# Routing and expert slots moved inside both arms of attention's branch, with their data in used halves of q, k and v

## The chip, the core and the metric

The kernel runs on one core of one Trainium2 chip. A core has a matrix engine (PE, TensorE), a vector engine (DVE, VectorE), an activation engine (ACT, ScalarE), a general engine (POOL, GpSimd) and a sequencer that issues transfers (SP, SyncE). Each works through its own list of instructions in order; semaphores tie the lists together. SP, ACT and POOL can issue DMA transfers, which sixteen DMA engines carry out. SBUF is the memory that the engines compute from, PSUM holds the products of PE, DRAM holds inputs, outputs and some scratch.

The metric is device time in microseconds (us), lower is better.

## The reference

The input is an image of 256 channels and 64 x 64 pixels, so 4096 tokens. Layer 0 is a windowed linear attention over the image and takes about the first 1000 us; the change leaves it alone. Layer 1 is:

```python
# --- layer 1 ---
t = _to_tokens(x)                                  # 4096 tokens x 256
t = t + attn(_ln_t(t))                             # 8 heads of 32, softmax over all 4096 keys
t = t + ffn(_ln_t(t))
x = _from_tokens(t, x)

def ffn(x):                                        # 8 experts, 256 -> 1024 -> 256
    logits = xt @ Wr + br
    probs = softmax(logits); top_p, top_idx = top_k(probs, 2)
    weights = top_p / top_p.sum(-1)
    xe = layernorm(xt) * ln_g[e] + ln_b[e]
    h = gelu(xe @ W1[e] + b1[e]); y = h @ W2[e] + b2[e]
    out = (weights[..., None] * y[of the two chosen experts]).sum(1)
```

Only the two chosen experts of a token are computed: the kernel sorts the tokens by expert on the chip ("routing") and runs the experts on groups of rows ("slots").

## The kernel before, in words

**Attention** stands in one arm of a branch, `with tc.If(tame > 0)` (L1271), taken when the scores are small enough for exponentials without a maximum; the `Else` arm holds a slower, safer attention. In the arm there are 16 rounds of 32 steps. A round is one chunk of 512 queries (`qc`, 8 of them) and one group of four heads (`g`, 2 of them); a step is one tile of 128 keys. In a step PE computes scores for four heads (`scores`, L1326) into one bank (`ps_one`) and a set of three (`ps_three`, two such sets in turn, `three_banks()`); ACT takes the exponential of the one bank (L1335) and of the three (L1338) into a buffer of 128 x 2048, of which there are eight; two steps later PE multiplies it with the values (`value_sums`, L1285). The softmax denominators need the sum of all these buffers: DVE adds most of them up (L1357), and every fourth buffer is added by a DMA from POOL instead (`pe<-pe`, L1346). A buffer is free again three steps after its own when DVE adds it, six steps when the DMA does. At the start of the next round DVE copies the finished sums out of PSUM (`take`, L1369); later steps of the next round pack the denominators, send them through DRAM (SP), and scale the result (L1407). In every odd round, at steps 13 and 25, two tiles each go through the output projection (`some_projections`, L1263), whose results DVE adds to the tokens `t` (L1267), with the statistics of the next layer norm.

**Early routing** (`early_routing`, L951) routes the first 12 tiles of tokens to four "early" slots, the first 256 of the rows for each of four experts, while attention still runs. Its data lie in the half of the queries that attention no longer needs. It is a list of parts: load; norms; top one; top two; count (two products with constant matrices on PE, in a `three_banks()` turn of their own, L1014, copied by DVE, L1016); ranks; places; one-hot tables; invert (24 small matmuls, again a turn of its own, L1042, copied at L1049); finish; and six parts that write the normed rows to DRAM (`zrows`). The table `when` (L1418) gives each part a whole step, `(8, 13), (8, 21), (8, 25), (9, 9), ...`; `tc.issue_after(latest[0])` puts it behind DVE's last add.

**After the branch** both arms meet, and a second part opens new pools (L1519): constants (L131) and the row `br` are loaded, the full routing runs on DVE, POOL and PE (two_norms, logits, best, counts L1715, ranks, one-hots L1803 to L1826), and the slots run beside it, dealt out by `advance(n)`, which takes `n` steps of the generator `run`. There are four early slots, 28 full ones of 256 rows and four half ones, 36 in all. For a slot, `load` fetches the expert's `cols`, `W1`, `W2`, `b2` through SP (L1566 to L1569, three buffers for the weights) and its rows through POOL (`xs`, an indirect gather, L1587); `enter` transposes them (L1602) and applies gain and shift (L1607 on ACT, L1611 on DVE); then 8 x 2 products with `W1` (L1632), Gelu on ACT (L1635), 2 x 8 products with `W2` (L1648), the bias on DVE (L1652), and an indirect scatter to `yrows` in DRAM (L1653). Slots beyond the usual number stand in a second branch, `If(more_slots)`, that is not taken here. The ending loads the two results of each token (`y<-yrows`, L1869), weighs and adds them, transposes (L1879) and stores the image.

No planner decides the order in attention: it is the order of the calls, shifted by `issue_after`. Each engine's list is in that order, and everything behind the branch's end waits for everything in it.

Of the kernel before, what the change touches and what calls it, by code (L numbers as in the profile page):

```python
# [30 lines left out]
P = 128  # L31
# [85 lines left out]
def tile_conv_attn_hybrid(ctx: ExitStack, tc: tile.TileContext, a: dict, out: bass.AP):  # L117
# [27 lines left out]
    class Norm:  # L145
# [8 lines left out]
        def stats(self, i):  # L154
            st6 = self.pool.tile([P, 6], F32, tag="st6", name="st6", bufs=2)
            nc.vector.bn_stats(st6, t[:, i, :C])
            nc.vector.bn_aggr(self.mv[:, i, :], st6)
# [735 lines left out]
    def rsqrts(x, y, part):  # L893
        bits = y.bitcast(I32)
        nc.vector.tensor_single_scalar(bits, x.bitcast(I32), 1, op=ALU.arith_shift_right)
        nc.vector.tensor_scalar(bits, bits, -1.0, float(0x5F3759DF), op0=ALU.mult, op1=ALU.add)
        for _ in range(3):
            nc.vector.scalar_tensor_tensor(part, y, -0.5, y, op0=ALU.mult, op1=ALU.mult)
            nc.vector.tensor_mul(part, part, x)
            nc.vector.scalar_tensor_tensor(y, part, 1.5, y, op0=ALU.add, op1=ALU.mult)  # L900

    def two_norms(first, last, x, y, part, less):
        mean, var = (z[:, first:last] for z in (norm2.mean, norm2.var))
        nc.vector.tensor_scalar_add(x[:, 0], var, 1e-5)
        nc.vector.scalar_tensor_tensor(x[:, 1], x[:, 0], 1e-5, var, op0=ALU.mult, op1=ALU.add)
        rsqrts(x, y, part)
        nc.vector.scalar_tensor_tensor(less, mean, -1.0, y[:, 1], op0=ALU.mult, op1=ALU.mult)

    def logits(to, first, last, rstd, br):
        shape = [P, last - first, NE]  # L910
        on_experts = lambda v: v.unsqueeze(2).to_broadcast(shape)
        on_tiles = lambda v: v.unsqueeze(1).to_broadcast(shape)
        nc.vector.tensor_mul(to, on_experts(norm2.mean[:, first:last]), on_tiles(wr_sum))
        nc.vector.tensor_sub(to, t[:, first:last, C:], to)
        nc.vector.tensor_mul(to, to, on_experts(rstd))
        nc.vector.tensor_add(to, to, on_tiles(br))

    def best(hot, most, first, place, logit, rank):
        shape = list(logit.shape)
        on_experts = lambda v: v.unsqueeze(2).to_broadcast(shape)  # L920
        nc.vector.tensor_reduce(most, logit, AX.X, ALU.max)
        nc.vector.tensor_tensor(first, logit, on_experts(most), ALU.is_equal)
        nc.vector.tensor_mul(first, first, rank.unsqueeze(1).to_broadcast(shape))
        nc.vector.tensor_reduce(place, first, AX.X, ALU.max)
        nc.vector.tensor_tensor(hot, first, on_experts(place), ALU.is_equal)

    def without(logit, hot):
        nc.vector.scalar_tensor_tensor(logit, hot, -1e30, logit, op0=ALU.mult, op1=ALU.add)

    def positions(hot, row, at, pos, whole, part, within, which, off):  # L930
        nc.vector.tensor_mul(at, hot, row.rearrange("p e i -> p i e"))
        nc.vector.tensor_reduce(pos, at, AX.X, ALU.add)
        if off:
            nc.vector.tensor_scalar_add(whole, pos, off)
        else:
            nc.vector.tensor_copy(whole, pos)
        nc.vector.tensor_single_scalar(part, whole, P - 1, op=ALU.bitwise_and)
        nc.vector.tensor_copy(within, part)
        nc.vector.tensor_single_scalar(whole, whole, 7, op=ALU.arith_shift_right)
        nc.vector.tensor_copy(which, whole)  # L940

    def rows_of(source, target, low, high, got, second, spare, spares):
        nc.vector.scalar_tensor_tensor(got, high, float(P), low, op0=ALU.mult, op1=ALU.add)
        nc.vector.tensor_scalar(second, got, N + 1.0, -float(N), op0=ALU.is_ge, op1=ALU.mult)
        nc.vector.tensor_add(second, second, got)
        nc.vector.tensor_scalar(source, second, -1.0, 0.0, op0=ALU.add, op1=ALU.max)
        nc.vector.scalar_tensor_tensor(spare, got, 0.0, spares, op0=ALU.is_equal, op1=ALU.mult)
        nc.vector.tensor_add(spare, spare, got)
        nc.vector.tensor_scalar_add(target, spare, -1.0)

    def early_routing(spaces, banks):  # L951

        M, E = ETILES, EARLY
# [14 lines left out]

        names = ["rank", "iota", "before", "ones", "number", "high", "base", "spare_early"]
# [28 lines left out]

        def norms():
            two_norms(0, M, x, y, part, less)  # L1000

        def top_one():
            logits(logit, 0, M, y[:, 0], br)
            best(hots[0], most, one, place, logit, c["rank"])

        def top_two():
            without(logit, hots[0])
            best(hots[1], most, one, place, logit, c["rank"])
            nc.vector.tensor_add(chosen.rearrange("p e i -> p i e"), hots[0][:, :, :E], hots[1][:, :, :E])
# [71 lines left out]
    with ExitStack() as phase:  # L1081
# [382 lines left out]
        with branch.Else():  # L1464


            with (
# [48 lines left out]
                for part in early_routing([qk[:, 0, g, :] for g in range(KC)], lambda n: [one_bank() for _ in range(n)]):  # L1516
                    part()

# [391 lines left out]
```

## Time and profile before

| | us |
|---|---|
| median of the runs (3) | 2788.68 |
| lowest, highest | 2784.85, 2788.74 |
| the profiled execution | 2792.98 |
| its span, first to last instruction | 2791.2 |
| granted clock of PE, mean | 0.981 |
| attention's steps (first to last exponential of the 16 rounds) | 1110 to 2212 |
| PE's first transposes of slot 0 | 2230.3 |
| last products of a slot | 2746 |

| engine | busy us | share |
|---|---|---|
| PE | 2666.9 | 96% |
| DVE | 1873.2 | 67% |
| ACT | 1512.3 | 54% |
| POOL | 817.1 | 29% |

A line of the profile in order of time reads: start, length, engine, line of the kernel, operation, what it writes and reads, the shapes, how many instructions it groups, and in brackets how long the engine sat idle before it and what ended that ("issue": nothing that the profile shows). A line of the table of stretches gives the busy time of each engine between two times. Busy shares are means over the whole kernel; a stage is read by its own rows. PEclk is the clock that PE was granted, in parts of full speed.

### The profile page before, as it was taken

Reading aid. Unit: us, or ns where it says so; the run is one execution under the profiler, and the core shown is the slowest. Engines: PE = TensorE matmul, PEld = TensorE weight load, DVE = VectorE, ACT = ScalarE, POOL = GpSimd, SP = SyncE. Lnnn points to the kernel's source line nnn. Section 1 sums busy time; section 2 is a strip of 40 time slices with the busy share of each in tenths; the row PEclk is TensorE's granted clock in tenths of the full one; section 3 lists DMA queues with packets and bytes.
Section 4 is the critical chain, followed back from the end, with each engine's and each line's share of the span. In section 5 each row is a group of like instructions: output and inputs, shape, how many; then the busy total and the mean of one; then the engine's idle time right before and its main releaser. Section 6 shows DMA issues by size and latency. Waiting matters only on the chain. (4 is left out here: it accounts for less than half of the span.)

```text
span 2791.2 us, 72155 instructions
## 1 busy us (share of the span) xinstructions
PE 2666.9 (96%) x31106; PEld 1221.1 (44%) x31106; DVE 1873.2 (67%) x2518; ACT 1512.3 (54%) x2110; POOL 817.1 (29%) x918
## 2 busy tenths in 40 slices
PE   6889999988999999999999999999999899999996
PEld 5454336645433655111212121212121278888884
DVE  6758688565878875888888888898888741111114
ACT  3322323222332334999898988898989642222222
POOL 2057777404877741000000100000000112222220
PEclk9999999999999999999999999999999999999996
DMA  5000000000000000555555555555655455665665
GB/s 143 6 23 25 11 28 21 8 12 23 22 13 28 21 21 1 107 111 118 109 121 109 116 111 111 105 117 105 128 118 117 97 196 190 209 198 197 212 211 191
DMA packets 120990, 266.04 MB, mean 95 GB/s; under 512 B 20659, under 2 KB 81817, under 8 KB 106581
## 3 DMA queue, kind: packets, MB, share of 16 engines
q0 software_dynamic: 22368, 133.18, 22.7%
q1 hardware_dynamic: 91124, 119.20, 13.1%
q10 hardware_dynamic: 7168, 8.92, 0.9%
q8 instruction: 248, 4.06, 0.6%
q14 instruction: 82, 0.66, 0.1%
HBM read 127.81 MB, written 18.12 MB: 52 GB/s over the span
## 5 line engine op out<-in xcount | busy, mean ns | idle before, releaser
L1326 PE MATMUL ps_three<-qk 32*64 32x512 f32 x6144 | 564.9, 614 | 3.2 <-DVE t L1267 1.3
L1326 PE MATMUL ps_one<-qk 32*64 32x512 f32 x2048 | 560.0, 614 | 0.2 <-ACT pe L1335 0.2
L1357 DVE TENSOR_TENSOR act<-act,pe 128x2048 f32<-128x2048 f32 x195 | 446.8, 2291 | 87.0 <-ACT pe L1338 53.4
L642 ACT COPY sm<-ps_sc 128x384 f32<-128x384 f32 (+3 forms) x454 | 218.4, 510 | 526.9 <-PE ps_sc L822 338.6
L1338 ACT ACTIVATE pe<-ps_three 128x1536 f32<-128x1536 f32 x330 | 477.4, 1447 | 0.0
L649 DVE TENSOR_TENSOR sm<-ps_sc,mask 128x512 f32<-128x512 f32 (+3 forms) x740 | 340.0, 519 | 68.8 <-PE ps_sc L822 65.6
L649 POOL TENSOR_TENSOR sm<-sm,mask 128x192 f32<-128x192 f32 (+3 forms) x428 | 349.6, 846 | 113.7 <-ACT sm L642 113.3
L1357 DVE TENSOR_TENSOR act<-act 128x2048 f32<-128x2048 f32 x150 | 344.8, 2299 | 55.5 <-ACT act L1338 42.0
L1346 POOL DMA_DIRECT2D pe<-pe x108 | 92.9, 860 | 949.6 <-ACT pe L1338 675.6
L1285 PE MATMUL ps_acc<-pe,v 128*32 128x512 f32 x2640 | 353.2, 607 | 0.0
L1635 ACT ACTIVATE hid<-ps_hp,cols 128x256 f32<-128x256 f32 (+1 forms) x288 | 133.0, 462 | 349.5 <-PE ps_hp L1632 347.6
L1326 PEld LDWEIGHTS ps_three<-qk 32*64 32x64 f32 x6144 | 112.8, 130 | 416.9 <-ACT pe L1335 242.2
L1338 ACT ACTIVATE act<-ps_three 128x1536 f32<-128x1536 f32 x182 | 263.2, 1446 | 0.0
L1632 PE MATMUL ps_hp<-xe,w 128*128 128x256 f32 (+1 forms) x1152 | 247.9, 371 | 0.0
L1648 PE MATMUL ps_yp<-w,hid 128*128 128x256 f32 x1088 | 241.1, 379 | 0.0
L822 PE MATMUL ps_sc<-qk 32*64 32x384 f32 (+3 forms) x3584 | 234.6, 458 | 0.1
L1335 ACT ACTIVATE pe<-ps_one 128x512 f32<-128x512 f32 x330 | 197.3, 598 | 61.3 <-PE ps_one L1326 37.1
L649 POOL TENSOR_TENSOR sm<-sm,ycut 128x384 f32<-128x384 f32 (+4 forms) x146 | 147.2, 1029 | 257.3 <-ACT sm L642 256.9
L1632 PEld LDWEIGHTS ps_hp<-xe,w 128*128 128x128 f32 x1152 | 201.8, 191 | 39.8 <-ACT hid L1635 5.2
L1648 PEld LDWEIGHTS ps_yp<-w,hid 128*128 128x128 f32 x1088 | 204.2, 190 | 26.5
L838 PE MATMUL ps_acc<-sm,v 128*32 128x256 f32 (+3 forms) x2688 | 213.3, 419 | 0.1
L1285 PE MATMUL ps_acc<-act,v 128*32 128x512 f32 x1456 | 193.9, 604 | 2.3 <-DVE act L1369 2.3
(335 smaller groups left out, 2882.0 us busy)
## 6 DMA issues: line engine op xcount, KB each, us to landing
pe<-pe POOLq DMA_DIRECT2D x108, 1024.0 KB
w<-in_L_ffn_W SPq DMA_DIRECT2D x72, 1024.0 KB
by<-recs SPq DMA_DIRECT2D x48, 256.0 KB
b<-in_L_ffn_b SPq DMA_DIRECT2D x36, 128.0 KB
rows<-in_x SPq DMA_DIRECT2D x16, 256.0 KB
y<-yrows SPq DMA_DIRECT2D x8, 512.0 KB
y<-yrows ACTq DMA_DIRECT2D x8, 512.0 KB
rec<-recs SPq DMA_DIRECT2D x60, 64.0 KB
```

Source lines behind the costliest of these rows:

```text
L642: copied = nc.scalar.copy(sm[:, :used], sc[:, :used])
L649: done = engine.tensor_mul(to, of, mk.unsqueeze(1).to_broadcast(list(to.shape)))
L822: nc.tensor.matmul(scs[h][u : u + rows, at : at + n], kT[hs[h], P * i + u : P * i + u + rows], qT[hs[h], CH * ix + CELL * c0 : CH * ix + C ...
L838: nc.tensor.matmul(acc[hs[h], CELL * c0 : CELL * c1], v[:, i, hs[h]], sms[h][:, at : at + n], start=not begun[0], stop=last and at == plac ...
L1285: nc.tensor.matmul(to[D * hd : D * (hd + 1), :], lhsT(hd), rhs(hd), start=start, stop=stop, skip_group_check=True,)
L1326: nc.tensor.matmul(to[CELL * u : CELL * (u + 1), :], qk[hs, 1, g, P * i + CELL * u : P * i + CELL * (u + 1)], qk[hs, 0, g, chunk(qc)], sta ...
L1335: first = nc.scalar.activation(head(pe, 0), one, AF.Exp, scale=C**-0.5)
L1338: nc.scalar.activation(pe[:, CH:], three.rearrange("p h n -> p (h n)"), AF.Exp, scale=C**-0.5).ins
L1357: latest[:] = [nc.vector.tensor_add(total, total, weights_of[r, i]).ins]
L1632: nc.tensor.matmul(hp[:, :n], w1[:, k, tok(m)], x_now[:, k, :n], start=k == 0, stop=k == KC - 1)
L1635: done["gelu"] = nc.scalar.activation(hid[:, m, :n], hp[:, :n], AF.Gelu, bias=cols[:, m : m + 1]).ins
L1648: product = nc.tensor.matmul(yp, hid[:, m, tok(j)], w2[:, m, :], start=m == 0, stop=m == NH - 1)
```

## The change

1. Routing and the slots leave the second part and become `route_and_run`, called inside both arms. Constants, `br`, the routing's small tiles and PSUM pools open there. The code stands twice in the program.
2. The slots' tiles no longer come from a pool. They are cut from q, k and v by `cutter`: three pairs of weights in the keys of group 0, the first four chunks of queries, and the keys of group 1; `xs`, `xe`, `b2`, `cols`, the lists of rows and the flags in query chunks 4 to 6; `hid` and `y` in the values. `next_of` rotates them. The ending's image lies in `act`.
3. `run` yields once after the loads of slot 0 and once after those of slot 1, before any PE work. These two yields are taken in attention's last round, at steps 0 and 29, behind `turned[0]`, the last small transfer of a round's reciprocals. The early slots' loads keep the order of SP's queue (`issue_after(done["weights"])`), and an early slot's bias comes ahead of its weights.
4. Early routing is cut into pieces of one or a few operations with a cost each, and dealt to rooms: steps 1, 9, 13, 17, 21 and 25 of rounds 8 to 14, each with so many us. A piece stands behind DVE's last add and behind `take`'s copy or the projection's last statistic. Count and inversion go into the third bank of a projection's set; the count's two results leave in one copy.
5. The flag `more_slots` is read behind the branch's end, after all slots.

```diff
-    with ExitStack() as phase:
-        wts = pool("m_wts", 1)
-        small = pool("m_small", 1)
-        cst.update(constants_of("m", wts))
-        br = row_on_all("L1_ffn_br", NE, wts)
...
-            w1 = work.tile([P, KC, HID], F32, name="w1", bufs=3)
-            w2 = work.tile([P, NH, C], F32, name="w2", bufs=3)
...
+        for_early = [qk[:, 0, g, : 4 * CH] for g in range(KC)]
+        of_keys = [(qk[:, 1, g, : 4 * CH], qk[:, 1, g, 4 * CH :]) for g in range(KC)]
+        of_queries = cutter([qk[:, 0, g, 4 * CH : 7 * CH] for g in range(KC)])
+        of_values = cutter([v.rearrange("p i c -> p (i c)")])
+        rotating = {
+            "w": [of_keys[0], for_early, of_keys[1]],
+            "xs": [of_queries(C) for _ in range(4)],
+            "xe": [of_queries(KC, SLOT) for _ in range(2)],
+            "b2": [of_queries(C) for _ in range(2)],
+            "cols": [of_queries(NH + 2 * KC) for _ in range(2)],
+            "hid": [of_values(NH, SLOT) for _ in range(2)],
+            "y": [of_values(C) for _ in range(4)],
+        }
+        def next_of(name):
+            rotating[name].append(rotating[name].pop(0))
+            return rotating[name][-1]
...
+                in_order = slot[0] and "weights" in done
+                with tc.issue_after(done["weights"]) if in_order else nullcontext():
+                    *of, done["weights"] = weights(slot)
...
+            ahead = [load(slots[0])]
+            yield
+            ahead.append(load(slots[1]))
+            yield
+            (ps,) = slot_ps
+            xe = enter(ahead[0], slots[0][0] is not None)
...
+        def route_and_run(work_on, slot_ps, beside, done):
+            with ExitStack() as experts:
+                wts, small = pool("m_wts", 1), pool("m_small", 1)
+                slot_ps.append(experts.enter_context(psum("m_ps", 2)))
+                cst.update(constants_of("m", wts))
+                br = row_on_all("L1_ffn_br", NE, wts)
...
-                when = [(8, 13), (8, 21), (8, 25), (9, 9), (9, 21), (10, 9), (10, 13), (10, 21), (10, 25), (11, 9), (11, 21), (12, 9)]
-                when += [(12, 13), (12, 21), (12, 25), (13, 9), (13, 21), (14, 9)]
-                early = dict(zip(when, early))
+                load_early, pieces = early_routing(for_early)
+                early, shared = {(8, 1): [load_early]}, {}
+                slots = [
+                    (r, i, room)
+                    for r in range(8, len(rounds) - 1)
+                    for i, room in ((1, 2.2), (9, 0.7), (13, 0.95), (17, 0.8), (21, 0.95), (25, 0.95))
+                ]
+                r, i, room = slots.pop(0)
+                for cost, ops in pieces:
+                    if cost is None:
+                        while not (r % KC == KC - 1 and i in (13, 25)) or (r, i) in early:
+                            r, i, room = slots.pop(0)
+                        shared[r, i] = ops
+                        r, i, room = slots.pop(0)
+                        continue
+                    if cost > room:
+                        r, i, room = slots.pop(0)
+                    room -= cost
+                    early.setdefault((r, i), []).extend(ops)
...
-                        some_projections(2)
+                        behind = some_projections(2, shared.get((r, i)))
...
                     if (r, i) in early:
-                        with tc.issue_after(latest[0]):
-                            early[r, i]()
+                        with tc.issue_after(latest[0]), tc.issue_after(behind.ins):
+                            all_of(early[r, i])
+                    if r == last and i in (0, NT - 3):
+                        with tc.issue_after(turned[0]):
+                            next(work_on)
...
+            route_and_run(work_on, slot_ps, beside, done)
         with branch.Else():
...
-            img = big.tile([P, KC, IMG, IMG], F32, name="img")
+            img = act.rearrange("p k (y x) -> p k y x", x=IMG)
```

## The prediction

> **What bounds the kernel now.** I read the stretch table first (busy time of each engine in stretches that I cut at the starts of attention's rounds), then the rows in order of time where a stretch is longer than its like, then the same around the end of attention and the end of the kernel.
>
> Rounds 6 to 14 of attention, one stretch per round. Columns: the stretch, its length, then busy us (instructions) of PE, PE's weight load, DVE, ACT, POOL, then PE's granted clock, DMA share and GB/s.
>
> ```profile
> core 0: us, PE busy (x) PEld busy (x) DVE busy (x) ACT busy (x) POOL busy (x), PEclk, DMA share, GB/s
> 1517.40:1583.90 66.50, 66.50 (x780) 12.93 (x776) 56.07 (x27) 62.53 (x67) 6.02 (x7) 1.00 0.57 116
> 1583.90:1654.40 70.50, 70.50 (x796) 15.81 (x792) 60.75 (x40) 62.58 (x67) 9.54 (x8) 1.00 0.56 113
> ...
> 1720.90:1797.80 76.90, 73.69 (x800) 16.56 (x796) 64.03 (x51) 62.46 (x66) 6.52 (x8) 0.98 0.54 109
> 1797.80:1864.40 66.60, 66.60 (x780) 12.94 (x776) 60.74 (x52) 62.63 (x67) 6.02 (x7) 1.00 0.55 112
> 1864.40:1937.40 73.00, 73.00 (x820) 17.51 (x816) 60.96 (x45) 62.57 (x67) 6.01 (x7) 1.00 0.54 110
> ```
>
> A step is one ACT pair of exponentials: 0.60 + 1.45 = 2.05 us, 32 of them 65.6, and every even round takes 66.5; PE is as full as ACT, DVE has 66.5 - 56.07 = 10.4 us free. An odd round also projects four tiles and takes 70.50 (round 7). Round 9 takes 76.90 and round 11 73.00: 6.4 and 2.5 us more than an odd round without early routing, 8.9 together. Round 10 carries 60.74 - 56.07 = 4.7 us of early routing on DVE and takes 66.60, so early work spread out there is free. The rows show what was not:
>
> ```profile
> 1726.56 1.06 PE L1285 MATMUL ps_acc<-act,v 128*32 128x512 f32 x8 [2.27 <-DVE act L1369]
> ...
> 1729.47 0.60 ACT L1335 ACTIVATE act<-ps_one 128x512 f32<-128x512 f32 x1 [3.08 <-PE ps_one L1326]
> ...
> 1771.11 0.65 PE L1014 MATMUL ps_three<-qk 128*128 128x48 f32 x4
> ...
> 1774.95 0.60 ACT L1335 ACTIVATE act<-ps_one 128x512 f32<-128x512 f32 x1 [2.67 <-PE ps_one L1326]
> ...
> 1910.78 1.62 PE L1042 MATMUL ps_three<-qk 128*128 128x16 bf16 x24
> ...
> 1914.47 0.60 ACT L1335 ACTIVATE act<-ps_one 128x512 f32<-128x512 f32 x1 [2.51 <-PE ps_one L1326]
> ```
>
> At 1726 PE waits for DVE's copy of the finished sums (L1369), which stands in DVE's queue behind adds that two bursts of early work (14 operations from 1700.90 to 1703.9, 9 from 1710.78 to 1713.4) had pushed back; ACT idles 3.08 us and 1.05 at the next step. At 1774 and 1914 the count (L1014) and the inversion (L1042) have taken a whole turn of the score banks, and their copy waits behind a 2.29 us add: 2.67 and 2.51 us of ACT.
>
> The end of attention:
>
> ```profile
> 2222.26 0.77 DVE L1267 TENSOR_TENSOR t<-ps_three,t 128x264 f32<-128x264 f32 x2 [0.30 <-PE ps_three L1263]
> ...
> 2224.10 0.37 SPq L131 DMA_DIRECT2D cstm<-in_constants  x1
> ...
> 2224.94 1.07 POOL L1587 DMA_INDIRECT xs<-zrows,lists  x1 [34.25 <-issue]
> ...
> 2227.01 0.30 DVE L904 TENSOR_SCALAR x_norms<-ln_mv 128x32 f32<-128x32 f32 x1 [3.10 <-issue]
> ...
> 2239.33 0.66 PE L1602 MATMUL ps_tp<-cst,xs 128*128 128x128 f32 x2 [3.69 <-DMA xs<-zrows,lists]
> ...
> 2243.45 0.81 PE L1632 MATMUL ps_hp<-xe,w 128*128 128x256 f32 x3
> ```
>
> The last sum lands at 2223.03. Then every engine leaves the branch and waits for all of it: DVE's taken jump is the 3.10 us of "issue". Only then come constants, weights and gathers. The DMA queues are full (0.96 of 16 engines from 2230.3 to 2243.5), and from 2243.45 PE does not stop:
>
> ```profile
> 2230.30:2243.50 13.20, 6.90 (x21) 4.52 (x22) 7.62 (x20) 2.84 (x5) 6.08 (x10) 0.51 0.96 341
> 2243.50:2301.00 57.50, 57.50 (x258) 45.05 (x257) 25.50 (x79) 27.75 (x57) 7.00 (x7) 1.00 0.53 175
> 2301.00:2746.00 445.00, 444.95 (x2170) 381.94 (x2168) 57.09 (x127) 123.24 (x267) 117.89 (x120) 1.00 0.58 193
> ```
>
> So the experts' 502 us are PE's, and what shifts the point of 2243.45 shifts all behind it. At the kernel's end the last rows go out at 2747.25, and the loads of the ending start when they have landed:
>
> ```profile
> 2747.25 0.97 POOL L1653 DMA_INDIRECT yrows<-y,target  x1 [3.05 <-DVEq L1850]
> 2751.62 1.48 SPq L1869 DMA_DIRECT2D y<-yrows  x3
> ```
>
> **The change, part by part.** *Early routing.* It takes away 8.9 us (above). It adds, inside two projections of odd rounds, the count's 0.65 us and the inversion's 1.62 us of PE, with one copy each (0.2 and 0.17 us) behind adds that DVE makes there anyway: 2.6 us, all on the path, since PE is full in a round. The pieces on DVE number 0.17 to 0.30 us each; they stand after every third big add, in at most 0.95 us (2.2 after the copy of the sums at step 1), and are over by round 12. Four steps last 8.2 us and hold three adds of 2.29 plus a gap each, about 7.2, so 0.95 just fits; their cover is DVE's 10.4 us per round, and each piece without it would cost itself, about 18 us in all. Best end: the copies vanish, -6.6. Worst: one late copy of the sums per round with pieces, at the 3.9 us of 1726, in five rounds: +13. Round 10's 66.60 is the nearest row: -6.3.
>
> *Weights and gathers of slots 0 to 2 during rounds 14 and 15.* Slot 0's two matrices start about 2122 and 2141, those of slot 1 and half of slot 2 about 2191, 1 MB each, on SP's queue behind the last small transfers of a round, so nothing of attention queues behind them on SP. The four gathers of slots 0 and 1 (about 1.1 us each) stand on POOL in round 12 ahead of the move of step 21 and wait for the last write of the normed rows, which starts after step 17. What all this may hurt are POOL's moves (L1346, 1 MB): their packets end 6.6 to 7.6 us after issue, and the buffer is wanted again six steps after its own began, 12.25 us less the 2.05 of the step itself, 10.2 after issue: 2.6 to 3.6 us of slack. The gathers, 4.4 us that begin about step 20, make one move late by about a microsecond, inside the slack. Beside weights the slack is used up: from 2226 to 2243, 1 MB of W1 took about 2.7 us of all engines and W2 about 4. Bounds: 0 (inside the slack) and +4 (three moves late by about 1.3). I take +1.
>
> The Trainium skill speaks against this step ("DMA: Bandwidth & Descriptors", Queues, rings and completion order): each DMA engine goes round the queues that have work, packet by packet. By it the move issued at 2189.82 gets half of the engines for the 5.9 us left at 2191.3, lands at about 2203 and is 3 us late for 2200; in the trace gathers beside weights (2231 to 2234) moved about 127 KB/us where a move alone has about 200, which lands it at 2200.6. The sum by the rule is 2 us worse than mine, by the row 0.4 better.
>
> *The passage.* Gone are the jump, the wait for the whole branch, and the loads. Constants are issued after the last scaling (about 2220.4 instead of 2224.10) and land about 2223; slot 0's transposes wait for the last sum, 2223.03; then those of slot 1, first products of slot 0, and slot 2's transposes, which wait for gathers that POOL issues after the freed rows and its 1.04 us cast of a constant: 2224.3 and 2225.5. The first gather of 2224.94 was through its packets about 3.3 us after its issue, while the queues were still empty, as they will be now: 2228.8. One pair of transposes later PE stands where it stood at 2243.45: 2229.4. That is -14.1. Best end: gathers hidden, PE limited by its own rows (four transposes 1.2, four more 1.2, products 1.7, four 1.2 after 2223.03, some 0.3 of ACT between): 2228.2, -15.3. Worst: gathers as slow as in the full queues (2231.69 to 2239.3, 7.6 us): 2233.7, -9.8. What comes next is late in no row: DVE's choices were ready at 2238.4 after starting at 2227.01, now about 2235.3, and PE wanted them at 2255.54, now 2241.4.
>
> *The slots* keep their order on PE, POOL, ACT and DVE; cost 0, covered by DMA's 0.58 share from 2301 to 2746. Bounds 0 and the rival below.
>
> *The end.* The jump now stands behind the last scatter. ACT, SP, DVE and PE make it while that lands (2748.22 to 2751.03). POOL's ends about 3.05 us after 2748.22, then its load of the flag: +0.7, bounds 0 and +3.
>
> The Trainium skill ("Runtime: NRT & Kernel Launch", Instruction fetch mechanics) says a taken branch out of the fetched window stalls until its page has come, and the longer arm lies there. It has no price for it; with the whole 3.10 of DVE's row uncovered the sum would be 2.4 us worse.
>
> Sum: -6.3 + 1 - 14.1 + 0.7 = -18.7 us. The profiled execution took 2792.98 us (span 2791.2, 1.8 around it), 4.3 above the median 2788.68; taken from its own time the sum gives 2774.3, and against the median of the runs 2770.0.
>
> **Rivals.** (a) *DVE's pieces push copies or adds back*, so attention gains nothing: 2776.3, with one or two late copies more up to 2783. For it: the 3.08 us at 1729 came from 5.4 us of such work. Against it: that came in two bursts late in a round, and round 10 took 4.7 us in portions up to 1.4 for nothing. (b) *The gathers or routing's chain on DVE become the limit of the passage*: half its 14.1 goes, 2777. For it: 6 us of slack are left to the choices. (c) *Slower: the slots stall.* The tiles now lie in halves of q, k and v that all slots share; if a load or gather waits for a reader of the slot before its own, PE stops once per slot. 36 slots: from 0.52 us each the gain is gone; at 1 us the time is 2806. Against it: PE's 444.95 of 445.00 us with DMA at 0.58, so a load may come half a slot late. (d) *The change gains little*: transfers in the last rounds delay attention by what the passage wins, 2783 to 2794.
>
> **How the numbers follow.** This kernel's runs tell 0.2%, 5.6 us, from no change. Forecast (2763 to 2775) 0.60; (a) 0.15; (b) 0.12, both faster; (d) 0.06, same; (c) 0.07, slower. Faster 0.87, same 0.06, slower 0.07. The low end takes the best ends together (-6.6 + 0 - 15.3 + 0 = -21.9, 2766.8) and the 4 us between runs; the high end reaches over (a) and (b) to 2783.
>
> **What would show it.** Round 9 (count) at about 71.4, round 11 (inversion) at 72.3, even rounds at 66.5, rounds 14 and 15 within 2 us of 66.5 and 71.3; slot 0's transposes on PE about 2218 (2223.1 less attention's 5.3), no DVE "issue" of 3 us there; some 500 us of full PE after; 4 to 5 us from last scatter to first load. Wrong: idle PE between slots, waits for L1369's copy or for moves, or a new idle stretch before the counts.

## The result, and the profile after

| | before | after |
|---|---|---|
| median of 6 runs each, us | 2787.89 | 2777.89 |
| lowest, highest | 2784.39, 2788.74 | 2772.1, 2780.61 |
| the profiled execution | 2792.98 | 2777.12 |
| its span | 2791.2 | 2775.3 |
| granted clock of PE, mean | 0.981 | 0.986 |

After to before is 0.9963, with an interval of 0.995 to 0.9976: faster by 10.0 us. The forecast was 18.7 us. The time lies inside the range, but nearly 9 us of the expected gain are missing, and the rest of this part looks for them.

The table of stretches of the changed kernel, one line per round, rounds 9 to 14 (stretch, length, then busy us of PE, its weight load, DVE, ACT, POOL, then granted clock, DMA share, GB/s):

```profile
1713.80:1784.70 70.90, 70.90 (x800) 16.24 (x796) 63.29 (x59) 62.52 (x66) 6.77 (x8) 1.00 0.58 118
1784.70:1851.20 66.50, 66.50 (x780) 12.92 (x776) 59.84 (x44) 62.53 (x66) 6.02 (x7) 1.00 0.55 112
1851.20:1923.30 72.10, 72.10 (x820) 17.25 (x816) 61.77 (x53) 62.66 (x67) 6.02 (x7) 1.00 0.56 115
1923.30:1998.50 75.20, 70.20 (x780) 13.33 (x776) 59.72 (x38) 62.52 (x66) 15.77 (x11) 0.95 0.54 119
1998.50:2069.00 70.50, 70.50 (x796) 15.80 (x792) 59.09 (x40) 62.56 (x66) 5.99 (x7) 1.00 0.59 119
2069.00:2135.50 66.50, 66.50 (x780) 12.90 (x776) 56.26 (x28) 62.58 (x66) 6.03 (x7) 1.00 0.61 129
```

Rounds 9 and 11 (first and third line) are what early routing was to win: PE is busy for the whole of both. Round 12 (fourth line) is new: an even round that takes 75.20 instead of 66.5, with PE idle for 5 us, and POOL busy for 15.77 us where the other rounds have 6 to 7. The rows of that stretch in order of time, DVE's and POOL's, then one of PE and three of ACT:

```profile
1970.88 2.29 DVE L1770 TENSOR_TENSOR act<-act 128x2048 f32<-128x2048 f32 x1 [1.07 <-ACT act L1751]
1971.69 2.44 POOL L1389 DMA_INDIRECT qk<-zrows,lists  x1 [8.69 <-DMA rec<-recs]
1973.28 2.29 DVE L1770 TENSOR_TENSOR act<-act,pe 128x2048 f32<-128x2048 f32 x1
1974.43 2.02 POOL L1389 DMA_INDIRECT qk<-zrows,lists  x1 [0.30 <-issue]
1975.68 2.29 DVE L1770 TENSOR_TENSOR act<-act 128x2048 f32<-128x2048 f32 x1
1976.75 2.04 POOL L1389 DMA_INDIRECT qk<-zrows,lists  x1 [0.30 <-issue]
1979.05 2.29 DVE L1770 TENSOR_TENSOR act<-act,pe 128x2048 f32<-128x2048 f32 x1 [1.07 <-ACT pe L1751]
1979.10 3.06 POOL L1389 DMA_INDIRECT qk<-zrows,lists  x1 [0.30 <-issue]
1982.17 1.02 POOL L1759 DMA_DIRECT2D pe<-pe  x1
...
1989.37 0.60 ACT L1748 ACTIVATE pe<-ps_one 128x512 f32<-128x512 f32 x1 [6.20 <-DMA pe<-pe]
...
1990.02 1.97 PE L1739 MATMUL ps_one<-qk 32*64 32x512 f32 x4 [5.00 <-ACT pe L1748]
...
1992.07 0.60 ACT L1748 ACTIVATE act<-ps_one 128x512 f32<-128x512 f32 x1 [0.75 <-PE ps_one L1739]
...
1996.01 0.60 ACT L1748 ACTIVATE pe<-ps_one 128x512 f32<-128x512 f32 x1 [2.01 <-PE ps_one L1739]
```

The four gathers of slots 0 and 1 hold POOL from 1971.69 to 1982.16. Behind them stands the move (L1759) that frees a score buffer; it goes out at 1982.17, lands 7.1 us later, and ACT has waited 6.20 us for that buffer (the idle time in brackets names the move as what ended it). PE stops with it, for 5.00 us. That is 6.2 of the round's 8.7 us. The other 2.5 come behind it: from 1988.80 to 1995.63 the granted clock of PE is 0.50, and ACT waits another 0.75 and 2.01 us, now for PE's scores.

The passage from attention to the slots, rows in order of time:

```profile
2215.14 0.34 SPq L131 DMA_DIRECT2D cstm<-in_constants  x1
2216.87 0.77 DVE L1677 TENSOR_TENSOR t<-ps_three,t 128x264 f32<-128x264 f32 x2 [0.30 <-PE ps_three L1673]
2217.74 1.06 PE L1404 MATMUL ps_tp<-cst,qk 128*128 128x128 f32 x8 [0.91 <-PE ps_three L1673]
2219.07 1.99 PE L1438 MATMUL ps_hp<-qk 128*128 128x256 f32 x8 [0.27 <-ACT qk L1409]
2222.59 0.41 PE L1404 MATMUL ps_tp<-cst,qk 128*128 128x128 f32 x2 [1.53 <-DMA qk<-zrows,lists]
2223.75 0.44 PE L1404 MATMUL ps_tp<-cst,qk 128*128 128x128 f32 x2 [0.75 <-DMA qk<-zrows,lists]
2224.03 7.03 PE L1438 MATMUL ps_hp<-qk 128*128 128x256 f32 x24
```

DVE's last sum ends at 2217.64 and PE transposes slot 0 from 2217.74, 0.1 us later; before, PE's first transposes came 7.3 us after the last sum. PE then waits 1.53 and 0.75 us for the rows of slot 2. From 2224.03 it does not stop any more, which is 6.39 us after the last sum; before it was 20.42 (2223.03 to 2243.45). The passage is shorter by 14.03 us.

The stretches behind it, and the kernel's end:

```profile
2224.03:2231.00 6.97, 6.97 (x27) 5.74 (x26) 5.76 (x15) 3.44 (x8) 0.96 (x2) 0.76 0.12 36
2231.00:2290.00 59.00, 59.00 (x264) 46.19 (x263) 25.90 (x80) 26.20 (x54) 9.82 (x10) 1.00 0.45 145
2290.00:2730.00 440.00, 440.00 (x2138) 371.51 (x2137) 56.65 (x125) 120.27 (x261) 114.99 (x117) 1.00 0.59 193
```

```profile
2731.32 0.97 POOL L1459 DMA_INDIRECT yrows<-v,qk  x1 [2.53 <-DVE v L1458]
2736.19 8.29 SPq L1982 DMA_DIRECT2D y<-yrows  x5
```

PE is full from 2224 to 2730. In the first of these stretches it ran at 0.76 of its clock, and its 24 products took 7.03 us. Between the last scatter and the first load of the ending lie 4.87 us.

**Where the 15.9 us between the two spans went.** Each term is read from the same two rows of both traces.

| part | before, us | after, us | difference |
|---|---|---|---|
| layer 0, up to attention's first exponential (untouched) | 1110.27 | 1104.82 | -5.5 |
| round 0 (untouched) | 66.59 | 64.96 | -1.6 |
| round 9 | 76.97 | 70.93 | -6.0 |
| round 11 | 72.99 | 72.02 | -1.0 |
| round 12 | 66.56 | 75.27 | +8.7 |
| the other rounds | | | 0.0 |
| last sum to the first of the 24 products | 20.42 | 6.39 | -14.0 |
| these 24 products | 5.35 | 7.03 | +1.7 |
| 11th to last bias sum of the slots | 405.22 | 407.51 | +2.3 |
| last bias sum to the end | 45.21 | 44.73 | -0.5 |

The first two lines are work that the change doesn't touch. Other executions show both values of round 0: of nine profiled executions of the changed kernel and its variants one has 66.59, the others 64.96 or 64.97; layer 0 takes 1103.6 to 1106.6 us in the nine. The execution of before that was profiled lay 5.1 us above its median, and the one of after 0.8 below its own, so of the 15.9 us 5.9 are chance between these two, and 10.0 remain. The same sum by parts: without the first two lines, -8.8.

### The profile page after: what moved, and what is told of

Same layout as the page of the kernel before. It is cut to its first block, busy times and chain, and to the rows that moved or that the text cites. A ratio compares the mean times of both kernels' runs of the same rounds, so it can differ in the third digit from the quotient of the medians.

```text
span 2775.3 us, 72311 instructions
## 1 busy us (share of the span) xinstructions
PE 2661.1 (96%) x31106; PEld 1212.8 (44%) x31106; DVE 1873.0 (67%) x2517; ACT 1512.8 (55%) x2110; POOL 822.4 (30%) x918
## 3 DMA queue, kind: packets, MB, share of 16 engines
q1 hardware_dynamic: 91124, 119.20, 13.1%
## 4 chain that ended last, share of the span: by engine, by line
PE 91%; DMA 3%; DVE 3%; issue 2%; POOL 1%; ACT 0%; ACTq 0%; SPq 0%; DVEq 0%; POOLq 0%
PE ps_three L1739 18%; PE ps_acc L1698 18%; PE ps_hp L1438 8%; PE ps_sc L822 8%; PE ps_yp L1454 8%; PE ps_acc L838 7%; PE ps_sc L722 3%; PE ps_sc L749 3%; PE ps_acc L780 3%; PE ps_two L407 2%; PE ps_two L440 2%; PE ps_mm L1238 2%; DMA yrows<-v,qk 2%; PE ps_two L521 1%; PE ps_acc L768 1%
## 5 line engine op out<-in xcount | busy, mean ns | idle before, releaser
L1770 DVE TENSOR_TENSOR act<-act,pe 128x2048 f32<-128x2048 f32 x195 | 446.8, 2292 | 84.9 <-ACT pe L1751 53.0
L1770 DVE TENSOR_TENSOR act<-act 128x2048 f32<-128x2048 f32 x150 | 344.9, 2299 | 57.2 <-ACT act L1751 44.0
L1759 POOL DMA_DIRECT2D pe<-pe x108 | 93.1, 862 | 933.1 <-ACT pe L1751 653.5
L1441 ACT ACTIVATE v<-ps_hp,qk 128x256 f32<-128x256 f32 (+1 forms) x288 | 133.1, 462 | 343.8 <-PE ps_hp L1438 341.9
L1438 PE MATMUL ps_hp<-qk 128*128 128x256 f32 (+1 forms) x1152 | 249.7, 373 | 0.3 <-ACT qk L1409 0.3
L1454 PE MATMUL ps_yp<-qk,v 128*128 128x256 f32 x1088 | 241.0, 379 | 0.0
L1748 ACT ACTIVATE pe<-ps_one 128x512 f32<-128x512 f32 x330 | 197.4, 598 | 66.5 <-PE ps_one L1739 36.1
L1438 PEld LDWEIGHTS ps_hp<-qk 128*128 128x128 f32 x1152 | 197.2, 190 | 47.4 <-ACT v L1441 13.1
L1454 PEld LDWEIGHTS ps_yp<-qk,v 128*128 128x128 f32 x1088 | 204.2, 190 | 26.5
```

The lines of the kernel that those rows point to most:

```text
L1438: nc.tensor.matmul(hp[:, :n], w1[:, k, tok(m)], x_now[:, k, :n], start=k == 0, stop=k == KC - 1)
L1441: done["gelu"] = nc.scalar.activation(hid[:, m, :n], hp[:, :n], AF.Gelu, bias=cols[:, m : m + 1]).ins
L1454: product = nc.tensor.matmul(yp, hid[:, m, tok(j)], w2[:, m, :], start=m == 0, stop=m == NH - 1)
L1748: first = nc.scalar.activation(head(pe, 0), one, AF.Exp, scale=C**-0.5)
L1770: latest[:] = [nc.vector.tensor_add(total, total, weights_of[r, i]).ins]
```

## The experiments

All edits are made to the changed kernel, and from the second on to the kernel of the first experiment, unless it is said otherwise. Four of the kernels share one set of runs of the kernel before (median 2787.51: gathers late, half the dose, own tiles, the first thick portions), four another (2788.85), on another chip; across the two, ratios are compared.

### The gathers of slots 0 and 1 behind attention's last move

If round 12 is lost to the four gathers ahead of a move on POOL, putting them behind the last of the moves has to give it back.

```diff
-                return *of, xs
+                return (*of, gather_rows(slot)) if gathered else of
...
-            ahead.append(load(slots[1]))
+            ahead.append(load(slots[1], False))
+            with tc.issue_after(done["move"]) if "move" in done else nullcontext():
+                ahead = [(*of, gather_rows(slot)) for of, slot in zip(ahead, slots)]
             yield
...
-                        nc.gpsimd.dma_start(buffers[sums_of[r, other]], pe, accum_op=ALU.add)
+                        done["move"] = nc.gpsimd.dma_start(buffers[sums_of[r, other]], pe, accum_op=ALU.add).ins
```

> The changed kernel, but the four row gathers of slots 0 and 1 stand on POOL behind the last buffer move of round 15 instead of ahead of the move of step 21 in round 12. Theory (the gathers hold POOL for 10.5 us, the next move is 10 us late, its buffer is missed): round 12 takes 66.5 us instead of 75.3, PE's slot work begins 8.7 us earlier, and the median falls from 2777.9 to about 2769. Rival (round 12 is slow because the last write of the normed rows and the small transfers delay things, or the gathers cost as much wherever they stand): round 12 stays over 72 us, or round 15 or the passage loses what round 12 wins, and the median stays at 2775 to 2778.

Median 2766.95 us (2766.01 to 2772.63), 0.9934 [0.9921, 0.9948] of before, 10.9 us less than the changed kernel. Round 12 as a stretch, and POOL's rows, first the move that had been late, then the gathers in their new place:

```profile
1922.00:1988.60 66.60, 66.60 (x780) 12.95 (x776) 59.51 (x38) 62.58 (x65) 6.02 (x7) 1.00 0.63 136
```

```profile
1969.74 0.86 POOL L1764 DMA_DIRECT2D pe<-pe  x1 [7.42 <-DMA pe<-pe]
...
2175.57 1.07 POOL L1392 DMA_INDIRECT qk<-zrows,lists  x1 [0.30 <-issue]
2176.95 1.96 POOL L1392 DMA_INDIRECT qk<-zrows,lists  x1 [0.30 <-issue]
2179.22 2.05 POOL L1392 DMA_INDIRECT qk<-zrows,lists  x1 [0.30 <-issue]
2181.57 2.10 POOL L1392 DMA_INDIRECT qk<-zrows,lists  x1 [0.30 <-issue]
```

Round 12 is an even round again. The move is issued 47.2 us after its round's start; in the changed kernel that would have been 1970.5, and it came at 1982.17, 11.7 us late: the first gather began 1.2 us after the move was due, and the four took 10.5. Here the move lands at 1976.85, and ACT begins to fill its buffer at 1982.49, so it had 5.6 us of slack. 11.7 less 5.6 is 6.1, and ACT's wait in the changed kernel was 6.20.

```profile
2214.83 5.34 PE L1443 MATMUL ps_hp<-qk 128*128 128x256 f32 x24
```

The 24 products that took 7.03 us take 5.34 here, at a granted clock of 1.00, after waits of nearly the same length (1.61 and 0.89 us). In the four other profiled executions that keep these two waits (1.36 to 1.83 and 0.73 to 0.84 us) they take 5.35. The 1.7 us more in the changed kernel's profile belong to that execution, not to the change.

Why a gather lasts 2 to 3 us is read from the traces of all nine kernels of the changed form. They have 44 gathers that are issued while attention runs. 41 of them begin while an add of DVE (L1770, two inputs of 128x2048, 2.29 us) is under way, and every one of these ends 0.82 to 0.95 us after that add ends: in the rows of round 12 the adds end at 1973.17, 1975.57, 1977.97 and 1981.34 and the gathers at 1974.13, 1976.45, 1978.79 and 1982.16. The three that begin in a gap between adds last 0.95 to 1.07, though an add starts 0.17 to 0.34 us later. The 128 to 132 indirect transfers of each kernel that come after attention last 0.95 to 1.19. So a gather that starts beside an add behaves as if it did nothing until the add is over. The moves that POOL issues beside the same adds are not held up: in the changed kernel 95 of 110 begin during an add, and none takes more than 1.12 us (row of the page of the changed kernel: line, operation, count, busy us, mean ns):

```profile
L1759 POOL DMA_DIRECT2D pe<-pe x108 | 93.1, 862 | 933.1 <-ACT pe L1751 653.5
```

The Trainium skill ("SBUF — State Buffer", Who interferes with whom) says that a VectorE instruction with two SBUF inputs contends with a GpSimd instruction that reads SBUF, through ports that the two share as an exclusive lock, and that the order of issue decides who waits. The 41 gathers agree with that. That a gather in its turn holds up an add no row shows: the three adds that start 0.17 to 0.34 us into a gather take 2.26 to 2.29 us, like the others. The same section infers that such an instruction doesn't hold up the writing of a transfer's descriptors; for the moves that fits, for the gathers these rows say the opposite. What in a gather needs the port no run here shows.

### Half the dose

```diff
-            ahead = [load(slots[0], False)]
+            ahead = [load(slots[0])]
...
-                ahead = [(*of, gather_rows(slot)) for of, slot in zip(ahead, slots)]
+                ahead[1] = (*ahead[1], gather_rows(slots[1]))
```

> Only slot 1's two gathers late, slot 0's two as in the changed kernel in round 12. Theory (POOL's time counts: two gathers take about 5 us, the move is 5 us late where 2.6 to 3.6 are free): round 12 loses 1.5 to 3.5 us instead of 8.7. Rival (what delays the move is the wait for the written rows, however many gathers follow): round 12 loses 7 to 9 us as with four.

A single run took 2767.82 us. Rows of POOL in round 12, and one of ACT:

```profile
1970.64 2.40 POOL L1392 DMA_INDIRECT qk<-zrows,lists  x1 [8.72 <-DMA rec<-recs]
1973.35 2.02 POOL L1392 DMA_INDIRECT qk<-zrows,lists  x1 [0.30 <-issue]
1975.37 1.02 POOL L1764 DMA_DIRECT2D pe<-pe  x1
...
1984.02 0.60 ACT L1753 ACTIVATE pe<-ps_one 128x512 f32<-128x512 f32 x1 [1.93 <-PE ps_three L1744]
```

Two gathers put the same move at 1975.37 instead of 1969.4, 6.0 us late, and it takes 8.6 us to land instead of 7.1: it lands at 1983.94, 7.5 us late. Less the 5.6 us of slack that is 1.9. ACT waits 1.93 us and goes on 0.08 us after the landing (the row names PE, but it is the move's landing that comes just before). Round 12 takes 68.36 and round 13 70.81, 2.1 us lost together. PE idles for 0.74 us at the most here, its clock stays at 1.00, and nothing like the 2.5 us behind the stop in the changed kernel follows. So the lateness of the move's landing counts, beyond 5.6 us, and not that gathers run in this round.

### Gelu's results in tiles of their own

The slots take 2.3 us more, 0.07 per slot, and PE's products show no wait. Both kernels' rows of the line that applies Gelu, with ACT's own semaphore instructions below it (ACTq) and who waited for it; first before, then after:

```profile
L1635 ACT ACTIVATE hid<-ps_hp,cols x288: 367/473/481, 2241.7 to 2739.1; 128x256 f32<-128x256 f32 x128, 128x128 f32<-128x128 f32 x16
L1635 ACTq EVENT_SEMAPHORE  x33: 17/8207/8207, 2273.4 to 2724.8; - x33
...
  PEld ps_hp L1632: 5.2, 33
```

```profile
L1441 ACT ACTIVATE v<-ps_hp,qk x288: 367/474/477, 2221.7 to 2723.7; 128x256 f32<-128x256 f32 x128, 128x128 f32<-128x128 f32 x16
L1441 ACTq EVENT_SEMAPHORE  x254: 17/17/8128, 2255.6 to 2723.7; - x127
...
  PEld ps_hp L1438: 13.1, 83
```

The Gelu itself is as long as before (median 474 ns and 473). But ACT now has 254 semaphore instructions on this line instead of 33, and PE's weight loads wait for it 83 times and 13.1 us instead of 33 times and 5.2. The results used to go into tiles that a pool hands out anew for each slot; now they go into two cuts of `v` that are written again and again, and 222 of the 288 Gelus got a second wait, beside the one for PE: on the semaphore that ACT's own Gelus raise. The Gelu before has ended by then, since ACT sits idle for some 0.4 us ahead of each. The wait still shows: between 2400 and 2690 us a Gelu starts 84 ns (median) after PE has raised its semaphore; before the change it is 23 ns. The edit gives the results two pool tiles again, once routing's own tiles are done with:

```diff
+        own_hid = []
...
-                hid = next_of("hid")
+                hid = own_hid[0].tile([P, NH, SLOT], F32, name="hid") if own_hid else next_of("hid")
...
+                own_hid.append(experts.enter_context(tc.tile_pool(name="m_hid", bufs=2)))
                 for _ in work_on:
                     pass
+                own_hid.pop()
```

> The gathers late, and the Gelu results of all slots after the routing in fresh tiles of a pool instead of rotating cuts of the values. Theory (each Gelu waits for the Gelu before it because the cut is written again and again, its bank comes free some 65 ns later, PE waits 0.01 to 0.02 us at each of eight column blocks): 0.07 us less per slot from the fifth slot on, 2.2 us in all beside the gain of the late gathers: about 2767. Rival (weights read from cuts of q and k, or bias and gains there, slow the products themselves): the slots keep their 0.07 us each, and the median is that of the late gathers alone, about 2769.

Median 2764.47 us (2762.6 to 2765.05), 0.9917 [0.9904, 0.9931] of before, 2.5 us less than with the first edit alone. The same view:

```profile
L1448 ACTq EVENT_SEMAPHORE  x34: 17/8207/9851, 2245.8 to 2697.1; - x34
...
  PEld ps_hp L1445: 4.5, 29
```

All but 34 of the semaphore instructions are gone, a Gelu starts 23 ns after PE's semaphore again, and the slots take 405.21 us from the 11th bias sum to the last, against 405.22 before the change and 407.51 with the first edit alone. The edit changes the place of the tiles along with the waits; no run parts the two, but the delay of each Gelu goes with the waits. This is the fastest kernel of the study: it beats the changed one by some 13 us and the one before by 23.

### Nothing loaded ahead

Does the passage's gain come from the loads that run during attention, or from the branch that engines no longer have to leave? Here the weights of slots 0 and 1 are issued behind the constants, after attention. Their rows are not: the four gathers keep their order behind the last move, and begin between 2177.32 and 2185.12, in attention.

```diff
-                    if r == last and i in (0, NT - 3):
-                        with tc.issue_after(turned[0]):
-                            next(work_on)
...
                 br = row_on_all("L1_ffn_br", NE, wts)
+                with tc.issue_after(loaded[0]):
+                    next(work_on)
+                    next(work_on)
```

> The gathers late, and the weights of slots 0 and 1 loaded behind the constants, after attention, instead of during rounds 14 and 15. Theory (the passage was won by both: the branch's join and jump gone, and the weights already there): W1 of slot 0 lands about 5 us after its issue, beside the constants, slot 2's gathers share the queues with 4 MB of weights and take 6 to 7 us instead of 3.6; the 24 products that follow start 4 to 6 us later than with the gathers late alone, about 2772. Rival 1 (the early weights are nearly all of the passage's 14 us): 10 to 13 us later, 2777 to 2780. Rival 2 (the join alone counted): under 2 us later, about 2768.

Median 2776.88 us (2773.74 to 2778.54), 0.9958 [0.9943, 0.9974] of before. The passage:

```profile
2209.48 1.06 PE L1409 MATMUL ps_tp<-cst,qk 128*128 128x128 f32 x8 [0.91 <-PE ps_three L1683]
...
2217.95 0.66 PE L1409 MATMUL ps_tp<-cst,qk 128*128 128x128 f32 x2 [7.40 <-DMA qk<-zrows,lists]
...
2219.45 6.88 PE L1445 MATMUL ps_hp<-qk 128*128 128x256 f32 x26
```

From attention's last exponential to the 11th bias sum it is 121.1 us, against 114.8 with the loads ahead: 6.3 us, within which PE ran the 26 products at a clock of 0.78 (stretch 2217.95 to 2226.30), about a microsecond of the 6.3. So the weights ahead are worth some 6 of the 14.0 us of the passage. The other 7.7, by subtraction, go with the engines staying in the arm and with the rows of slots 0 and 1 ahead (they are on PE at 2209.48 in this build too); the runs do not part these two. What PE waits for in this build are slot 2's rows, which share the DMA engines with the weights (DMA share 0.87 from 2209.48 to 2217.95, 0.92 in the stretch behind it).

### The rows of slots 2 and 3 ahead as well

The waits of 1.5 and 0.8 us that remain in the passage are for rows of slot 2. With eight cuts for rows instead of four, these can be gathered with the others; the transposed rows move to `v` to make room.

```diff
-            "xs": [of_queries(C) for _ in range(4)],
-            "xe": [of_queries(KC, SLOT) for _ in range(2)],
+            "xs": [of_queries(C) for _ in range(8)],
+            "xe": [of_values(KC, SLOT) for _ in range(2)],
...
+                in_time = [gather_rows(slot) for slot in slots[2:EARLY]]
```

> The gathers late, and eight row buffers instead of four (the transposed rows move to the values), so that the rows of slots 2 and 3 too come before attention ends. Theory (PE's two waits for slot 2's gathers, 1.6 and 0.9 us, are the last that holds the passage): from slot 0's first product to the 24 that follow it takes about 3 us instead of 5.2, four more transposes included, and the median would be about 2765. Rival (behind the gathers stands another wait, for ACT's table load and first Gelu): the 24 products start no earlier than before by more than 0.5 us.

A single run took 2774.28 us, 0.9948 of before against 0.9934 without the edit: slower, by the spans 8.3 us, of which 2.5 lie in layer 0. The waits for rows went as expected: the 24 products follow the first ones after 3.16 us instead of 5.18. But the fifth to the 11th bias sum now takes 50.18 us instead of 42.87, and the rows there are

```profile
2279.71 1.13 PE L1444 MATMUL ps_hp<-v,qk 128*128 128x256 f32 x4 [1.20 <-issue]
2284.16 0.47 ACT L1447 ACTIVATE v<-ps_hp,qk 128x256 f32<-128x256 f32 x1 [4.50 <-remote]
2284.69 2.07 PE L1444 MATMUL ps_hp<-v,qk 128*128 128x256 f32 x4 [3.84 <-issue]
```

ACT stands still for 4.50 us in the middle of a slot's Gelus, and PE behind it. The trace names nothing of this core that ended these waits ("remote" and "issue"), so the cause stays open. In the stretch from 2273 to 2280 POOL, which issues gathers for later slots, is busy for 5.29 us against 2.50 in the first experiment; whether that has to do with it no run shows. Both edits together, with Gelu's results in their own tiles:

> The gathers late, eight row buffers, and fresh tiles for the Gelu results. Theory: the gains add, 2764.5 less 1 to 2 us: about 2763. Rival (the rows ahead gain nothing behind ACT's first Gelu): 2764 to 2765.

Median 2768.23 us (2766.45 to 2769.35), 0.9926 [0.9912, 0.994] of before; without the rows ahead the ratio was 0.9917. The same part takes 46.20 us. That is 3.4 us more than without the rows ahead (42.79), and the gain that was expected (2763) did not come: what the rows ahead win in the passage is lost a slot later.

### Early routing in thick portions again

The pieces stay as they are, but the rooms that they are dealt to become few and large: first so that the bursts have 12 and 8 operations in round 8,

```diff
-                    for i, room in ((1, 2.2), (9, 0.7), (13, 0.95), (17, 0.8), (21, 0.95), (25, 0.95))
+                    for i, room in ((13, 0.95), (21, 3.1), (25, 2.6))
```

> The gathers late, and early routing's pieces dealt to steps 13 (0.95 us), 21 (3.1 us) and 25 (2.6 us) of a round instead of six small rooms. Theory (5 us of pieces at the end of a round push DVE's copy of the sums back, and PE waits for it at the start of the next): rounds 9 to 12 that follow a loaded round each begin with a loss of about 3 to 4 us, rounds 9 to 12 take 6 to 14 us more in all than with the gathers late alone. Rival (in the kernel before it was the count's and inversion's own turns that cost, and DVE's order does not matter): rounds 9 to 12 take the same as with the gathers late alone.

A single run took 2770.78 us; its span is 4.8 us longer than that of the first experiment, of which 2.5 lie in layer 0 and round 0. Round 9 takes 72.05 (+1.1), round 11 72.20 (+0.2) and round 15 72.23 (+1.0). The sign is as expected, the size isn't: 2.3 us together, and 1.3 in rounds 9 to 12, for which 6 to 14 were expected. Then with bursts of 14 and 9 operations at the steps where before had them:

```diff
-                    for i, room in ((1, 2.2), (9, 0.7), (13, 0.95), (17, 0.8), (21, 0.95), (25, 0.95))
+                    for i, room in ((13, 0.0), (21, 3.5), (25, 2.75))
```

> The gathers late, and pieces in bursts of 14 and 9 at steps 21 and 25 of round 8, the very bursts of the kernel before; later rounds get bursts of 13 and 7, 11 and 6. Theory (DVE's queue overflows its slack at a threshold between the 4.9 us of the bursts of 12 and 8, which cost 1.1 us, and the 5.4 of the kernel before, which cost 3.9): steps 2 and 3 of round 9 lose 2.5 to 4 us. Rival (in the kernel before something else made the copy late): they lose at most 1.5 us.

A single run took 2773.75 us. Round 9 takes 73.29 (+2.4), round 11 73.25 (+1.2), round 13 72.52 (+2.0), 5.6 us together; the 2.4 are just under the 2.5 to 4 of the theory, and above the 1.5 of the rival. The first steps of round 9:

```profile
1720.39 0.68 DVE L1787 COPY act<-ps_acc 128x512 f32<-128x512 f32 x1
1721.12 1.07 PE L1703 MATMUL ps_acc<-act,v 128*32 128x512 f32 x8 [2.29 <-DVE act L1787]
1723.39 0.60 ACT L1753 ACTIVATE act<-ps_one 128x512 f32<-128x512 f32 x1 [2.46 <-PE ps_one L1744]
```

This is the stall that before shows at 1726: PE waits for the copy of the finished sums (L1787), which stands in DVE's queue behind an add, and ACT waits for PE. With the pieces dealt thinly the same copy is in time. From 12 and 8 operations to 14 and 9 the loss in round 9 doubles, so there is little between enough room and a stall.

## Why the prediction was right, and where it was not

- **Early routing, -6.3.** Measured -7.0 (-6.0 in round 9, -1.0 in round 11). The signs were there: round 9 at 70.9 for 71.4, round 11 at 72.0 for 72.3, even rounds 66.5 apart from round 12. The cover of DVE's free 10.4 us held, and rival (a) did not come. The thick portions show that the copy of the sums was the right thing to watch: it is what comes late first. A burst ahead of round 9 like that of before costs 2.4 us by itself here; that the rest of the 6.0 came from the count's own turn is left by subtraction; the profile before has ACT idle for 2.67 us there, but no run took that turn away alone.
- **Weights and gathers in the last rounds, +1, bounds 0 and +4.** This is the step that failed: +8.7, outside its bounds. The weights were not the fault: rounds 14 and 15 take 66.50 and 71.26 as before. The four moves beside weights landed 8.1 to 9.9 us after their issue (the others from round 9 on after 6.9 to 9.2), within the 10.2 that the prediction gave the buffer. The sentence that failed is "The gathers, 4.4 us that begin about step 20, make one move late by about a microsecond, inside the slack." It took 1.1 us for a gather from rows after attention, where DVE has no long adds. Beside them the four lasted 10.5 us, and the move was 11.7 us late. Two more sizes were off: the slack of this move was 5.6 us and not 2.6 to 3.6, which made the loss smaller, and the sum has no term for PE's clock, which fell to 0.50 for 6.8 us behind the stop and made the loss 2.5 us larger. The mechanism (a move late, the slack, ACT out of buffers) and its place were right. The first experiment took this cost away alone: its profiled span is 11.1 us shorter, 8.7 of it here, 1.7 in the 24 products and 0.7 in layer 0. The dose experiment agrees with the slack of 5.6.
- **The weighing of the page on queues.** By half of the engines the last move would have landed 13.2 us after its issue, by the trace's rate 10.8. The weights came even closer behind it than supposed (2186.78, after a move issued at 2185.63), and it landed after 9.05 us. In the profile before, with no weights beside it, the same move (2189.82) landed after 9.42. So this move shows no delay by weights, and neither estimate holds for it. The two moves beside slot 0's weights do show one: 8.99 and 9.89 us, where the same two took 6.91 and 6.90 before.
- **The passage, -14.1.** Measured -14.0, with its marks: slot 0's transposes 0.1 us after the last sum, no issue of 3 us on DVE, two waits for slot 2's rows, full PE 6.39 us after the last sum for 6.4. That the transposes also came at 2217.74 for 2218 is luck: that time supposed attention shorter by 5.3 us; it was longer by 1.7, and layer 0 and round 0, which the change leaves alone, were shorter by 7.1 in this execution. Rival (b) did not come. The working ran the removal of the jump and the loads together; the fourth experiment gives 6.3 to the weights ahead and leaves 7.7 to the jump and the rows ahead together.
- **The slots, 0.** Measured +2.3. Rival (c) looked for a load or a gather that waits for a reader of the slot before, at 0.52 us per slot to turn the sign, and there was none. What came is the same reuse of cuts in another guise: a wait on ACT's own list, 0.07 us per slot. The groups in the trace of before would have shown the size of what to look for: 33 semaphore instructions for 288 Gelus.
- **The end, +0.7.** Measured -0.5; 4.9 us from last scatter to first load, for 4 to 5. The jump behind the last scatter costs nothing that shows.
- **The sum.** -18.7 plus 7.7 (gathers) plus 2.3 (slots), less 0.7 (early routing) and 1.2 (end) is -10.6; the medians differ by 10.0. The time lies in the range, but partly by luck: the upper part of the range stood for (a) and (b), and other losses filled it.
- **The chances.** The likeliest case, 2763 to 2775, did not come; the time fell where (a) and (b) had put theirs, at 2776 to 2777, but by neither. The outcome is nearest to (d), transfers that delay attention, at some 0.6 of the size that (d) gave it (8.7 of 14.1 us).

## What to carry to other kernels

The price of an operation is taken from rows where its neighbours do what they will do in the new place: a gather of 1.0 us is one of 2 to 3 beside long two-input adds of VectorE, and what is queued behind it pays. Before a transfer is put early, look at what stands behind it on the same queue and how much slack that has; here the same gathers cost 8.7 us ahead of a move and nothing behind the last one. A stop can cost more than its own length: 2.5 of the 8.7 us came behind it, while PE's clock was at 0.50. When tiles become hand-cut parts of a larger one, count the semaphore instructions per operation before and after: waits that are already met still took time here.

## What the runs showed of the hardware that was not expected

- Indirect gathers that start beside a two-input add of DVE end 0.82 to 0.95 us after the add (41 of 41), while the plain moves that POOL issues keep their 0.86 us in the mean, 1.12 at the most. The adds are not held up by gathers that started before them (3 of 3).
- A second semaphore wait on 222 of 288 Gelus, for an earlier Gelu that had already ended, went with a start 84 ns instead of 23 after PE's semaphore, and with 2.3 us of PE's time over the slots.
- After 5.00 us without work PE ran at a granted clock of 0.50 for 6.8 us in the middle of attention; after an idle time of 0.74 us at the same place in another kernel its clock stayed at 1.00.
- Layer 0, the same code in all, took between 1103.6 and 1106.6 us in nine executions of the changed form and 1110.3 in the one of before; round 0 has two lengths, 64.96 and 66.59.
- The first products after the passage ran at a granted clock of 0.76 in one execution and 1.00 in five others, after waits of about the same length.
